# Two-layer masked attention: layer 1's q, k, v weights turned by VectorE instead of TensorE, with layer 1's features in another order

## The chip, the cores and the metric

The kernel runs on one core of a Trainium2 chip. The metric is device time in microseconds (us) for one whole execution. The profiles are single executions taken by the hardware profiler; in them PE is TensorE's matmuls, PEld its weight loads, DVE is VectorE, ACT ScalarE, POOL GpSimd, SP SyncE (which here issues all transfers), and L12 means line 12 of the kernel.

## The reference, cut to what matters

x is 128 x 128 x 512 in float32 (128 graphs of 128 nodes, 512 features), adj a boolean mask per graph. Two attention layers, each followed by a residual and a layer norm:

```python
# layer 0: 4 heads of 64
q, k, v = split_heads(x @ Wq), split_heads(x @ Wk), split_heads(x @ Wv)
sim = where(adj, q @ k.T * 64 ** -0.5, -max_float)
x = layernorm(x + softmax(sim) @ v @ Wo + bo)
# layer 1: 8 heads of 64
h = (x - mean) * rsqrt(var + 1e-5) * gamma + beta
q, k, v = split(h @ w_qkv.T)              # w_qkv is 1536 x 512
scores = where(adj | eye, q @ k.T * 64 ** -0.5, -1e9)
x = layernorm(x + softmax(scores) @ v @ w_out.T + b_out)
```

The weights of layer 0 are stored with the contracted feature as the row. w_qkv and w_out of layer 1 are stored with the output as the row, so that a matmul, which contracts over partitions, needs them turned.

## The kernel before

**Tiling.** Two graphs make a group g (G = 2); there are 64 groups. The 512 features are four chunks of 128 partitions (KC = 4). Every projection (layer 0's q, k, v; layer 1's qk and v; both output projections) is computed on 2 x 2 blocks with seven block products instead of eight, in the Strassen-Winograd manner; `product_0`, `product` and `out_product` issue them by number (1 to 7). The sums of blocks of x that this needs are made by GpSimd (`halves_sums`, L320), the sums of blocks of the weights once, in the opening and steps 2 to 4 (`combine`, L211: four subtractions, by VectorE except for one half of layer 1's qk). Products that share a PSUM bank must wait until ScalarE or VectorE has read the bank in between (the table `INTO`, L331; "a", "f" and "c" are the banks).

**Order.** The order of all instructions on each engine is written out by hand: `opening` (L804), `step(s)` for s = 2 to 63 (L846), then `closing_a`, `closing_b` twice, and `last`. Each engine takes its instructions in this order. Step s works on several groups at once: layer 0's projections of group s, layer 0's scores of s - 1, its attention and output of s - 2, layer 1's projections of s - 3, its scores of s - 4, its attention and output of s - 5.

**Transfers.** SyncE issues all transfers, in program order. x of a group comes in twice: as rows (`load_rows`, L83, the residual) and in column quarters (`load_quarters`, L99): quarter a holds features 128a to 128a + 127, goes to partitions 32a to 32a + 31, and a piece is 128 floats (512 bytes). `transposed` (L111) turns these by VectorE's transposes of 32 x 32 blocks, which leaves partition 32a + i of chunk c with feature 128a + 32c + i; layer 0's weights are loaded to match (L127 to L130, in quarters of 32 partitions, 1 KB pieces). Layer 1's input takes another way: `turn` (L246) transposes blocks of the normed rows, a trip through DRAM (`put`, `fetch`) moves blocks between partitions, and `finish` (L284) applies gamma and beta. The last two groups skip the trip: `finish_direct` (L299) turns their rows on TensorE.

**Layer 1's weights.** `load_transposed` (L147) loads a block r of 128 rows of w_qkv (12 blocks) or w_out (4) into a spare buffer of 128 partitions with 2 KB rows, and puts a function into the list `setup`. When called, it turns the block by four TensorE transposes into one PSUM bank, which ScalarE (odd r) or VectorE (even r) copies into w1 or wo1. `prepare(n)` (L800) calls the next n of the list: in the opening ten are called ahead of layer 1's first weight sums, two more later, and the rest (gamma and beta, w_out) in step 2. The spare buffers are two of the row buffers' pairs, KQ, v1, xT1 and aT1.

**The opening's order of transfers** is: x of group 0 in quarters (four transfers), Wk, Wq, Wv (four each), w_qkv blocks 0 to 3, x of group 1 (x_1) in quarters, mask 0, blocks 4 and 5, Wo, blocks 6 to 9, rows of group 0, bias 0, blocks 10 and 11, gamma, beta, w_out (four), rows and mask of group 1, bias 1, rows and mask of group 2, x of group 2 (x_2) in quarters.

**The opening's order of work** on TensorE is: layer 0's products of group 0 (1, 2, then 5, 6, 3, 7, 4), scores of group 0, products of group 1 (1, 2, 6, 5, 7), the transposes pt of group 0's probabilities (L649, `blocks_direct`), products 3 and 4 of group 1; then step 2 begins with scores of group 1, `attend` of group 0 (L677), and `product_0(2, 1)`, which reads x_2 turned. VectorE's own order between scores and pt is: turn x_1, mask the scores (L583), maxima (L589), the sums of w_out of layer 0 (`weight_sums_out(0)`, L221), the add of product 2 (L490), two of the weight blocks, the reciprocal (L606), on which GpSimd's product with the probabilities (L607) waits.

Of the kernel before, what the change touches and what calls it, by code (L numbers as in the profile page):

```python
# [10 lines left out]
F32 = mybir.dt.float32  # L11
U8 = mybir.dt.uint8  # L12
AF = mybir.ActivationFunctionType
ALU = mybir.AluOpType
# [3 lines left out]
P = 128  # L18
D = 64
G = 2  # L20
# [3 lines left out]
SCALE = D ** -0.5  # L24
# [3 lines left out]
def kernel(ctx: ExitStack, tc: tile.TileContext, x, adj, wq, wk, wv, wo, bo,  # L28
                            gamma, beta, w_qkv, w_out, b_out, out):
    nc = tc.nc  # L30
# [40 lines left out]
    K0, K1 = HEADS[0] // 2, HEADS[1] // 2  # L71
    KQ = const.tile([P, 4, 2, G, K1, 32], F32, name="kq")

    spare_rows(five, "r", 2)
    spare_rows(five, "r", 2)
    kq_rows = KQ.rearrange("p a w b c j -> p (a w b c j)")
    spare.extend(kq_rows[:, i * E:(i + 1) * E] for i in range(4))
    for pool, tag in ((two, "v1"), (two, "v1"), (one, "xT1"), (one, "aT1")):
        spare_rows(pool, tag, 2)

    X, XT = {}, {}

# [58 lines left out]
        nc.tensor.matmul(ready[:, :P], ident, ident, start=True, stop=True, skip_group_check=True)  # L141

    w1 = const.tile([P, KC, 3 * INNER[1]], F32, name="w1")
    wo1 = const.tile([P, INNER[1] // P, E], F32, name="wo1")
    setup = []

    def load_transposed(dst, src, name, *which):  # L147
# [12 lines left out]
        for r in which:  # L160
            raw = spare.pop(0)
            nc.sync.dma_start(raw, src[r * P:(r + 1) * P, :])
            setup.append(lambda r=r, raw=raw: part(r, raw))

    transposed(0)
    load_transposed(w1, w_qkv, "w_qkv", 0, 1, 2, 3)
    load_quarters(1)
    load_mask(0)
    load_transposed(w1, w_qkv, "w_qkv", 4, 5)
    wo0 = const.tile([P, INNER[0] // P, E], F32, name="wo0")  # L170
    nc.sync.dma_start(wo0, wo.rearrange("(c p) f -> p c f", p=P))
    load_transposed(w1, w_qkv, "w_qkv", 6, 7, 8, 9)
    load_rows(0)
    bias0 = const.tile([P, E], F32, name="bias0")
    nc.sync.dma_start(bias0, bo[None, :].to_broadcast([P, E]))
    load_transposed(w1, w_qkv, "w_qkv", 10, 11)
    gb_raw = one.tile([2 * KC, P], F32, tag="sm2", name="gb_raw")
    gb = const.tile([P, 2 * KC], F32, name="gb")
    nc.sync.dma_start(gb_raw[:KC], gamma.rearrange("(c p) -> c p", p=P))
    nc.sync.dma_start(gb_raw[KC:], beta.rearrange("(c p) -> c p", p=P))  # L180

    def turn_gamma_beta():
        pt = mm_tile("gb_t")
# [7 lines left out]
    bias1 = const.tile([P, E], F32, name="bias1")  # L191
    nc.sync.dma_start(bias1, b_out[None, :].to_broadcast([P, E]))

    I1 = INNER[1]
    KH = KC // 2

    w1qk = w1[:, :, :2 * I1].rearrange("p c (h f) -> p c h f", h=2)
    w1v = w1[:, :, 2 * I1:].rearrange("p c (h f) -> p c h f", h=2)
    wsqk = const.tile([P, 3, KH, I1], F32, name="wsqk")
    wsv = const.tile([P, 3, KH, I1 // 2], F32, name="wsv")  # L200

    def weight_sums(w, ws, *blocks_):

# [9 lines left out]
        for o, a, b in ((b12, b12, b11), (t2, b22, b12), (t3, t2, b11), (t4, b21, t2)):  # L213
            eng.tensor_tensor(o, a, b, op=ALU.subtract)  # L214

    def weight_sums_0(t):
        combine(*(w0[:, c:c + KH, t, h] for c in (0, KH) for h in range(2)), *(ws0[:, i, :, t] for i in range(3)))

    WSO = tuple(const.tile([P, 3, i // P // 2, E // 2], F32, name=f"wso{l}") for l, i in enumerate(INNER))

# [25 lines left out]
    def turn(g):  # L246
        if not 0 <= g < NG:
            return
        t = one.tile([P, 4, G * KC * 32], F32, tag="turned", bufs=2, name=f"turned_{g}")
        for b in range(G):  # L250
            nc.vector.transpose(t.rearrange("p a (b c i) -> p a b c i", b=G, c=KC)[:, :, b],
                                R[g][:, b].rearrange("p (c a i) -> p a c i", a=4, i=32))
        SCR[1] = put(t, f"scr_{g}")

    def arrive(g):
# [28 lines left out]
    def finish(g, half):  # L284
# [11 lines left out]
        if half == 1:  # L296
            sums(1, g)

    def finish_direct(g):  # L299

        xT = XT[1, g] = one.tile([P, KC, T], F32, tag="xT1", name=f"xT1_{g}")
        for b in range(G):
            pt = mm_tile(f"ht{g}_{b}")
            for c in range(KC):
                nc.tensor.transpose(pt[:, c * N:(c + 1) * N], R[g][:, b, c * P:(c + 1) * P], ident)
            for c in range(KC):
                o, i = xT[:, c, b * N:(b + 1) * N], pt[:, c * N:(c + 1) * N]
                scale, bias = gb[:, c:c + 1], gb[:, KC + c:KC + c + 1]
                if b == 0:
                    nc.scalar.activation(o, i, AF.Identity, bias=bias, scale=scale)  # L310
                else:
                    nc.vector.tensor_scalar(o, i, scale, bias, op0=ALU.mult, op1=ALU.add)
# [410 lines left out]
    def roots(l, g):  # L723
        mv = MV[l, g]
        if l == 0:


            ve1, root = power(l, g, mv[:, :, 1], 1, EPS * EPS, 1.0 + EPS)
        else:
            ve1, root = power(l, g, mv[:, :, 1], 1, EPS)  # L730
        shift = two.tile([P, G], F32, tag="shift", name=f"shift{l}_{g}")
        nc.gpsimd.tensor_tensor(shift, mv[:, :, 0], root, op=ALU.mult)
        nc.gpsimd.tensor_scalar_mul(shift, shift, -1.0)  # L733

        def ratios():

            ratio = RATIO[g] = three.tile([P, G], F32, tag="ratio", bufs=5, name=f"ratio_{g}")
            _, root0 = power(l, g, mv[:, :, 1], 0, EPS)
            nc.gpsimd.tensor_tensor(ratio, ve1, root, op=ALU.mult)
            nc.gpsimd.tensor_tensor(ratio, ratio, root0, op=ALU.mult)  # L740

        def norms():
            for b in range(G):
                nc.scalar.activation(R[g][:, b], R[g][:, b], AF.Identity, bias=shift[:, b:b + 1],  # L744
                                     scale=root[:, b:b + 1])
            if l == 1:
# [57 lines left out]
    def opening():  # L804

        sums(0, 0)
        cleared(1, 0)

        for t in (1, 0, 2):
            if t == 0:  # L810
                for h in range(2):
                    nc.vector.tensor_scalar_mul(w0[:, :, 0, h, :], w0[:, :, 0, h, :], SCALE)
            product_0(0, 1, 2, ts=(t,))
            weight_sums_0(t)
        product_0(0, 5, 6, 3)
# [24 lines left out]
        weight_sums(w1qk, wsqk, 0)  # L840
        product_0(1, 3)
        prepare(2)
        product_0(1, 4)
        transposed(2)

    def step(s):  # L846
# [18 lines left out]
            exps(s, 0, 0)  # L865
        product_0(s, 1)
        exps(s, 0, *((0, 1) if s < 5 else (1,)))
        out_product(0, s - 2, 1, 2, *(() if s == 2 else (5,)))
        maxima(s, 1 if s == 4 else 2)
        product_0(s, 2)  # L870
        if s == 2:
            out_product(0, s - 2, 5, 6)
        normalised(s, 0)
        out_product(0, s - 2, *(() if s == 2 else (6,)), 3)
        exps(s, 1, 0)
        if s == 4:
            maxima(s, 2)
# [274 lines left out]
```

## Time and profile before

| | us |
|---|---|
| median of three runs | 2735.53 (2735.45 to 2735.92) |
| the profiled execution | 2737.01 |
| its span in the profile | 2735.2 |
| TensorE busy | 2720.4 (99%) |
| VectorE busy | 2027.1 (74%) |
| GpSimd busy | 1750.5 (64%) |
| ScalarE busy | 1503.3 (55%) |
| the transpose of a weight block's copy: VectorE L158, mean | 0.683 |
| the same, ScalarE L156, mean | 0.581 |
| VectorE's transpose of 128 x 512 (L118), mean | 0.686 |
| x_2's transfers, issue to landing | 6.5 to 8.0 |

The profiled execution is 1.8 us longer than its span, which is what lies ahead of the first and behind the last instruction. "Busy" is the time in which at least one instruction of the engine was under way. A row of a timeline gives start, length, engine, line, operation, output and inputs; a bracket behind it gives the time that the engine had stood idle and what ended it. The chain of waits follows, from the last instruction back, what released each one.

### The profile page before, as it was taken

Reading aid. Unit: us, or ns where it says so; the run is one execution under the profiler, and the core shown is the slowest. Engines: PE = TensorE matmul, PEld = TensorE weight load, DVE = VectorE, ACT = ScalarE, POOL = GpSimd, SP = SyncE. Lnnn points to the kernel's source line nnn. Section 1 sums busy time; section 2 is a strip of 40 time slices with the busy share of each in tenths; the row PEclk is TensorE's granted clock in tenths of the full one; section 3 lists DMA queues with packets and bytes.
Section 4 is the critical chain, followed back from the end, with each engine's and each line's share of the span. In section 5 each row is a group of like instructions: output and inputs, shape, how many; then the busy total and the mean of one; then the engine's idle time right before and its main releaser. Section 6 shows DMA issues by size and latency. Waiting matters only on the chain.

```text
span 2735.2 us, 47645 instructions
## 1 busy us (share of the span) xinstructions
PE 2720.4 (99%) x14943; PEld 1933.5 (71%) x14943; DVE 2027.1 (74%) x3671; ACT 1503.3 (55%) x4804; POOL 1750.5 (64%) x2311
## 2 busy tenths in 40 slices
PE   9999999999999999999999999999999999999999
PEld 8867767667677676676776766767767667677688
DVE  6777777777777777777777777777777777777765
ACT  3456465465564554655646546556465465564654
POOL 5575666666766656667566666676666666756664
PEclk9999999999999999999999999999999999999999
DMA  6567777777777777777777777777777777777742
GB/s 180 156 204 207 218 221 206 219 214 219 211 208 218 220 200 217 214 215 211 208 222 217 206 220 213 216 215 205 216 220 206 220 214 217 209 208 222 207 142 70
DMA packets 550283, 562.62 MB, mean 206 GB/s; under 512 B 55560, under 2 KB 468752, under 8 KB 550032
## 3 DMA queue, kind: packets, MB, share of 16 engines
q1 hardware_dynamic: 550032, 559.58, 71.9%
q8 instruction: 121, 1.98, 0.3%
q14 instruction: 130, 1.06, 0.1%
HBM read 300.95 MB, written 258.47 MB: 205 GB/s over the span
## 4 chain that ended last, share of the span: by engine, by line
PE 96%; DMA 2%; SPq 1%; ACT 0%; issue 0%; DVE 0%; POOL 0%; POOLq 0%; ACTq 0%; DVEq 0%
PE qka L363 16%; PE a L476 12%; PE oa L514 11%; PE qkf L363 8%; PE va L363 8%; PE av L677 6%; PE f L476 6%; PE of L514 6%; PE qkc L363 4%; PE vf L363 4%; PE c L476 3%; PE oc L514 3%; PE sc L548 2%; PE sc L554 2%; PE vc L363 2%; PE sc_a L554 2%
## 5 line engine op out<-in xcount | busy, mean ns | idle before, releaser
L598 ACT ACTIVATE sm<-sm,nmax 128x128 f32<-128x128 f32 x1536 | 595.0, 393 | 1.6 <-DVE nmax L589 1.2
L607 POOL TENSOR_TENSOR sm<-sm,rec 128x1024 f32<-128x1024 f32 x192 | 364.1, 1897 | 340.8 <-DVE rec L606 337.4
L699 POOL TENSOR_TENSOR r<-r,bias 128x1024 f32<-128x1024 f32 x128 | 301.2, 2354 | 128.3 <-ACT r L698 128.3
L518 DVE TENSOR_TENSOR r<-oa,r 128x256 f32<-128x256 f32 x508 | 212.1, 417 | 161.6 <-PE oa L514 124.9
L598 ACT ACTIVATION_READ_ACCUMULATOR sm<-sm,nmax 128x1 f32 x1536 | 294.7, 192 | 0.0
L373 ACT COPY ev<-va 128x256 f32<-128x256 f32 x128 | 47.6, 372 | 432.5 <-PE va L363 432.5
L625 DVE STREAM_TRANSPOSE turnedp<-sm 128x1024 f32<-128x1024 f32 x188 | 233.4, 1242 | 62.4 <-POOL sm L607 57.9
L718 POOL TENSOR_SCALAR ve<-mv 128x2 f32<-128x2 f32 x191 | 41.4, 217 | 370.7 <-DVE mv L711 360.2
L744 ACT ACTIVATE r<-r,shift,root 128x512 f32<-128x512 f32 x254 | 193.0, 808 | 87.8 <-POOL shift L733 87.8
L589 DVE TENSOR_REDUCE nmax<-sm 128x8 f32<-128x1024 f32 x192 | 226.7, 1207 | 0.3
L363 PE MATMUL qkf<-w,xs 128*128 128x512 f32 x472 | 221.8, 592 | 0.0
L363 PE MATMUL qka<-wsqk,xs 128*128 128x512 f32 x472 | 221.8, 592 | 0.0
L514 PE MATMUL of<-wo,so 128*128 128x256 f32 x760 | 205.7, 379 | 0.3 <-DVE r L518 0.3
L514 PE MATMUL oa<-wso,so 128*128 128x256 f32 x760 | 205.6, 379 | 0.0
L326 POOL TENSOR_TENSOR xs<-xT 128x256 f32<-128x256 f32 x256 | 188.1, 735 | 24.3 <-DVE xT L118 19.8
L428 ACT ACTIVATE qo<-kq 128x512 f32<-128x512 f32 x118 | 67.9, 622 | 227.9 <-DMA kq<-scrkq 227.9
L476 PE MATMUL f<-w,xs 128*128 128x384 f32 (+1 forms) x512 | 181.1, 476 | 0.2 <-DVE w L214 0.2
L476 PE MATMUL a<-ws,xs 128*128 128x384 f32 (+1 forms) x512 | 181.0, 476 | 0.0
L583 DVE COPY_PREDICATED sm<-m,sc 128x512 f32<-128x512 uint8 x256 | 172.6, 728 | 11.2 <-PE sc L548 2.6
L710 DVE BATCH_NORM_STATS2 st<-r 128x6 f32<-128x512 f32 x254 | 174.9, 689 | 2.2
L569 POOL MEMSET sm<- 128x1024 f32 x192 | 175.1, 951 | 1.4 <-DVE turnedp L625 1.4
L514 PEld LDWEIGHTS oa<-wso,so 128*128 128x128 f32 x760 | 143.7, 190 | 45.7 <-issue 0.7
(181 smaller groups left out, 6340.3 us busy)
## 6 DMA issues: line engine op xcount, KB each, us to landing
scrp<-turnedp SPq DMA_DIRECT2D x188, 512.0 KB, 3.5
pT<-scrp SPq DMA_DIRECT2D x752, 128.0 KB, 2.9
kq<-scrkq SPq DMA_DIRECT2D x236, 256.0 KB, 4.8
x<-in_x_dram SPq DMA_DIRECT2D x256, 128.0 KB, 3.9
r<-in_x_dram SPq DMA_DIRECT2D x64, 512.0 KB, 4.2
out_dram<-r SPq DMA_DIRECT2D x63, 512.0 KB, 3.6
scr<-turned SPq DMA_DIRECT2D x62, 512.0 KB, 6.7
kq<-scr SPq DMA_DIRECT2D x248, 128.0 KB, 2.8
```

The source lines that it names most:

```text
L326: nc.gpsimd.tensor_tensor(o, a0, a1, op=op)
L363: nc.tensor.matmul(o, lhsT, rhs, start=first and m == 0, stop=m == len(todo) - 1, skip_group_check=True)
L476: nc.tensor.matmul(o, lhsT, rhs, start=first and n == 0, stop=n == len(todo) - 1, skip_group_check=True)
L514: nc.tensor.matmul(acc, left[:, c], right[:, c], start=first and c == 0, stop=c == hk - 1, skip_group_check=True)
L518: nc.vector.tensor_add(part, acc, part)
L569: nc.gpsimd.memset(sm, NEG1 if part else NEG0)
L589: nc.vector.tensor_reduce(NMAX[part], SM[part], AX.X, ALU.max, negate=True)
L598: nc.scalar.activation(sm[:, i, k, :], sm[:, i, k, :], AF.Exp, bias=nmax[:, i, k:k + 1], accum_out=total[:, i, k:k + 1])
L607: nc.gpsimd.tensor_tensor(SM[part], SM[part], rec[:, :, :, None].to_broadcast([P, 2, K1, N]), op=ALU.mult)
L625: nc.vector.transpose(t.rearrange("p q (h r) -> p q h r", r=32), SM.pop(part).rearrange("p i k (q r) -> p q (i k) r", r=32))
L699: nc.gpsimd.tensor_tensor(R[g], R[g], (bias0, bias1)[l][:, None, :].to_broadcast([P, G, E]), op=ALU.add)
L744: nc.scalar.activation(R[g][:, b], R[g][:, b], AF.Identity, bias=shift[:, b:b + 1], scale=root[:, b:b + 1])
```

## The change

It has four parts.

- **w_qkv** is loaded in column quarters, as x is: `load_blocks` issues four transfers for a range of blocks, each to 32 partitions in pieces of 128 floats, and VectorE turns each block with one transpose instruction straight into w1. Blocks 0 to 3 come into KQ, 4 to 9 (before wo0) into the place of the weight sums wsqk, 10 and 11 into that of wsv. w_out is loaded and turned as before.
- **Layer 1's features** take the order that this leaves: partition 32a + i of chunk c holds feature 128a + 32c + i. `turn`, gamma and beta, and `finish_direct` follow; the latter reads a copy by chunks that ScalarE makes (`by_chunk`) right after the norm of the last two groups.
- **The opening's weight sums of layer 0** are issued one by one: of each four, those that the next product needs come first, and the scaling of Wq is moved ahead of the last two sums of Wk's.
- **Step 2** issues layer 0's output products in the order that the later steps have.

```diff
-    spare_rows(five, "r", 2)
-    spare_rows(five, "r", 2)
-    kq_rows = KQ.rearrange("p a w b c j -> p (a w b c j)")
-    spare.extend(kq_rows[:, i * E:(i + 1) * E] for i in range(4))
-    for pool, tag in ((two, "v1"), (two, "v1"), (one, "xT1"), (one, "aT1")):
-        spare_rows(pool, tag, 2)
+    for _ in range(2):
+        spare_rows(two, "v1", 2)
...
+    def load_blocks(home, lo, hi):
+
+        n = (hi - lo) * P // 32
+        raw = home[:, :n * P].rearrange("p (m f) -> p m f", f=P)
+        rows = w_qkv[lo * P:hi * P].rearrange("(m j) (a f) -> a j m f", j=32, a=4)
+        for a in range(4):
+            nc.sync.dma_start(raw[32 * a:32 * a + 32], rows[a])
+
+        def part(r):
+            nc.vector.transpose(w1[:, :, r * P:(r + 1) * P].rearrange("p c (m j) -> p m c j", j=32),
+                                raw[:, (r - lo) * 4:(r - lo + 1) * 4].rearrange("p m (c i) -> p m c i", i=32))
+
+        setup.extend(lambda r=r: part(r) for r in range(lo, hi))
+
     transposed(0)
-    load_transposed(w1, w_qkv, "w_qkv", 0, 1, 2, 3)
+    load_blocks(KQ.rearrange("p a w b c j -> p (a w b c j)"), 0, 4)
     load_quarters(1)
     load_mask(0)
-    load_transposed(w1, w_qkv, "w_qkv", 4, 5)
+    load_blocks(wsqk.rearrange("p i c f -> p (i c f)"), 4, 10)
     wo0 = const.tile([P, INNER[0] // P, E], F32, name="wo0")
     nc.sync.dma_start(wo0, wo.rearrange("(c p) f -> p c f", p=P))
-    load_transposed(w1, w_qkv, "w_qkv", 6, 7, 8, 9)
     load_rows(0)
     bias0 = const.tile([P, E], F32, name="bias0")
     nc.sync.dma_start(bias0, bo[None, :].to_broadcast([P, E]))
-    load_transposed(w1, w_qkv, "w_qkv", 10, 11)
+    load_blocks(wsv.rearrange("p i c f -> p (i c f)"), 10, 12)
...
-    nc.sync.dma_start(gb_raw[:KC], gamma.rearrange("(c p) -> c p", p=P))
-    nc.sync.dma_start(gb_raw[KC:], beta.rearrange("(c p) -> c p", p=P))
+    for i, of_feature in enumerate((gamma, beta)):
+        nc.sync.dma_start(gb_raw[i * KC:(i + 1) * KC].rearrange("c (a i) -> c a i", i=32),
+                          of_feature.rearrange("(a c i) -> c a i", a=4, i=32))
...
-    def weight_sums_0(t):
-        combine(*(w0[:, c:c + KH, t, h] for c in (0, KH) for h in range(2)), *(ws0[:, i, :, t] for i in range(3)))
+    def weight_sums_0(*which):
+
+        for t, i in which:
+            b11, b12, b21, b22 = (w0[:, c:c + KH, t, h] for c in (0, KH) for h in range(2))
+            t2, t3, t4 = (ws0[:, j, :, t] for j in range(3))
+            o, a, b = ((b12, b12, b11), (t2, b22, b12), (t3, t2, b11), (t4, b21, t2))[i]
+            nc.vector.tensor_tensor(o, a, b, op=ALU.subtract)
...
             nc.vector.transpose(t.rearrange("p a (b c i) -> p a b c i", b=G, c=KC)[:, :, b],
-                                R[g][:, b].rearrange("p (c a i) -> p a c i", a=4, i=32))
+                                R[g][:, b].rearrange("p (a c i) -> p a c i", a=4, i=32))
...
+    def by_chunk(g, b):
+
+        if b == 0:
+            BY_CHUNK[g] = one.tile([P, G, KC, P], F32, tag="xT0", name=f"by_chunk_{g}")
+        nc.scalar.copy(BY_CHUNK[g][:, b].rearrange("p c (a i) -> p a c i", i=32),
+                       R[g][:, b].rearrange("p (a c i) -> p a c i", a=4, i=32))
...
-                nc.tensor.transpose(pt[:, c * N:(c + 1) * N], R[g][:, b, c * P:(c + 1) * P], ident)
+                nc.tensor.transpose(pt[:, c * N:(c + 1) * N], BY_CHUNK[g][:, b, c], ident)
...
+            if l == 0 and g >= NG - 2:
+                for b in range(G):
+                    by_chunk(g, b)
...
-        for t in (1, 0, 2):
-            if t == 0:
-                for h in range(2):
-                    nc.vector.tensor_scalar_mul(w0[:, :, 0, h, :], w0[:, :, 0, h, :], SCALE)
-            product_0(0, 1, 2, ts=(t,))
-            weight_sums_0(t)
+        product_0(0, 1, 2, ts=(1,))
+        weight_sums_0((1, 0), (1, 1))
+        for h in range(2):
+            nc.vector.tensor_scalar_mul(w0[:, :, 0, h, :], w0[:, :, 0, h, :], SCALE)
+        product_0(0, 1, 2, ts=(0,))
+        weight_sums_0((0, 0), (2, 0))
+        product_0(0, 1, 2, ts=(2,))
+        weight_sums_0((0, 1), (2, 1), (1, 2), (0, 2), (2, 2), (1, 3), (0, 3), (2, 3))
         product_0(0, 5, 6, 3)
...
-        out_product(0, s - 2, 1, 2, *(() if s == 2 else (5,)))
+        out_product(0, s - 2, 1, 2, 5)
         maxima(s, 1 if s == 4 else 2)
         product_0(s, 2)
-        if s == 2:
-            out_product(0, s - 2, 5, 6)
         normalised(s, 0)
-        out_product(0, s - 2, *(() if s == 2 else (6,)), 3)
+        out_product(0, s - 2, 6, 3)
```

More of the change, by code (lines that the diff above doesn't have):

```diff
@@ L143 @@
     w1 = const.tile([P, KC, 3 * INNER[1]], F32, name="w1")
+    I1 = INNER[1]
+    KH = KC // 2
+    wsqk = const.tile([P, 3, KH, I1], F32, name="wsqk")
+    wsv = const.tile([P, 3, KH, I1 // 2], F32, name="wsv")
     wo1 = const.tile([P, INNER[1] // P, E], F32, name="wo1")
@@ L192 @@
     nc.sync.dma_start(bias1, b_out[None, :].to_broadcast([P, E]))
-    I1 = INNER[1]
-    KH = KC // 2
     w1qk = w1[:, :, :2 * I1].rearrange("p c (h f) -> p c h f", h=2)
     w1v = w1[:, :, 2 * I1:].rearrange("p c (h f) -> p c h f", h=2)
-    wsqk = const.tile([P, 3, KH, I1], F32, name="wsqk")
-    wsv = const.tile([P, 3, KH, I1 // 2], F32, name="wsv")
     def weight_sums(w, ws, *blocks_):
@@ L297, in finish @@
             sums(1, g)
+    BY_CHUNK = {}
+    def by_chunk(g, b):
[3 more added lines that the diff above has]
+                       R[g][:, b].rearrange("p (a c i) -> p a c i", a=4, i=32))
     def finish_direct(g):
```

## The prediction

> **What bounds the kernel now.** I read the page first (busy shares, chain of waits), then the chain and the VectorE timeline of the first 45 us, then a table of stretches for the transfers, then SyncE's waits.
>
> ```profile
> PE 2720.4 (99%) x14943; PEld 1933.5 (71%) x14943; DVE 2027.1 (74%) x3671; ACT 1503.3 (55%) x4804; POOL 1750.5 (64%) x2311
> PE 96%; DMA 2%; SPq 1%; ACT 0%; issue 0%; DVE 0%; POOL 0%; POOLq 0%; ACTq 0%; DVEq 0%
> ```
>
> TensorE is busy in 99% of the span and makes 96% of the chain: whatever it gains or loses in the opening stays to the end. From 16 us on the opening's chain has no gap:
>
> ```profile
> 23.73 1.28 PE sc L548 x16
> ...
> 27.88 0.87 PE w_qkvt L152 x8
> ...
> 34.52 0.87 PE pt L649 x8
> ...
> 40.23 1.02 PE av L677 x16
> 41.26 1.55 PE a L476 x12
> ```
>
> (start, length, what.) Each block of weights that TensorE turns (L152) costs eight records and 0.87 us on the chain for two blocks. So TensorE looks like the bound here. But look at who only just arrives:
>
> ```profile
> 27.62 0.42 DVE L214 TENSOR_TENSOR wo<-wo 128x256 f32<-128x256 f32 x1
> 39.36 1.30 DVE L118 STREAM_TRANSPOSE xT<-x 128x512 f32<-128x512 f32 x2 [1.43 <-DMA x<-in_x_dram]
> ```
>
> Group 2's x is turned at 39.36, after VectorE had stood 1.43 us waiting for its transfer; it ends at 40.66, and product_0(2, 1), which reads it, starts at 41.2. TensorE has 0.5 us of slack against a transfer at the tail of the opening's queue. That queue is full:
>
> ```profile
> 5.00:11.50 6.50, 2.71 (x21) 2.36 (x21) 5.02 (x8) 0.00 (x0) 3.98 (x5) 0.97 1.11 227
> 11.75:14.50 2.75, 2.75 (x15) 2.75 (x14) 1.40 (x4) 0.30 (x1) 0.00 (x0) 0.51 1.04 371
> 14.75:17.30 2.55, 2.39 (x21) 2.20 (x20) 2.08 (x5) 0.48 (x1) 0.00 (x0) 1.00 1.22 193
> 17.50:28.50 11.00, 11.00 (x104) 10.63 (x104) 6.92 (x11) 3.31 (x9) 3.04 (x4) 1.00 1.04 381
> 28.50:38.50 10.00, 10.00 (x93) 10.00 (x92) 6.13 (x12) 5.94 (x21) 7.24 (x6) 1.00 0.83 203
> SPq L162 <- DMA r<-in_x_dram: 2.3, 1, 2.3
> ```
>
> (stretch, length, five engines' busy us, granted clock, DMA share, GB/s; last line from SyncE's waits.) The share is above 1 until 28.5 us. The rate goes by the form of the load: w0 in 32-partition quarters 227 GB/s, x_1 in quarters of 512-byte pieces (with a mask) 193, loads of 128 partitions with 2 KB rows 371 to 381. SyncE holds each transfer until the eighth before it has landed (the last line: w_out's third block waited for row tile 0, eight earlier), so x_2, the 48th to 51st, can't overtake.
>
> **What the skill says.** The Trainium skill, "SBUF — State Buffer", Door 1: The DMA port swizzle: partitions 0 to 31 reach 8 of the 16 ports; it gives 189 GB/s at 1 MiB with a limit near 218, against 328 and 436 for 128 partitions. The trace agrees: 193 to 227 against 371 to 381. "DMA: Bandwidth & Descriptors", Specifications, puts the smallest piece for line rate at 512 B, so it would see no loss from the pieces alone; here piece and quarter come together, and the measured quarter rate is used. "TensorE: Matmul & The Clock Gate", Part 1, says that idle time halves the clock until some 3.4 us of work have passed; the trace agrees: after the gap that ends at 11.2 the granted clock is 0.5 until 14.3, which cost about 1.65 us.
>
> **The change, part by part** (profiled execution: span 2735.2, its own time 2737.0; the median of the runs is 2735.5, and I add the difference to that).
>
> *TensorE's transposes go*: six pairs at 0.87, -5.2 us. Their copies (VectorE six at 0.68, ACT six at 0.58) go too; twelve VectorE transposes of 128x512 come, at 0.69 by the L118 row: VectorE +4.1 us net. They lie on VectorE's in-order queue between work that TensorE waits for: beside r0, r1 the add of product 7, which gates product 4 (0.6 to 1.2 us of TensorE waiting), and r4, r5 ahead of L606's reciprocal.
>
> *Opening's sums*: the scaling of Wq starts when Wq lands (9.9) instead of after four sums (10.6), -0.7; product 5 no longer waits for the sums of v, -0.4. Together -1.1.
>
> Without transfers in the way TensorE would finish scores(1) at 23.4 (before 25.0). The next chain is maxima, w_out's sums, the add, two transposes, reciprocal, GpSimd's product: 25.95 + 2.1 + 0.56 + 1.4 + 0.2 + 1.9 = 32.1 for the transposes pt (before 34.4), and 37.7 at the end of attend(2) (before 41.2): -3.5 us at most, since VectorE's chain takes the rest.
>
> *The transfers*: 3.15 MB of w_qkv change from rows to quarters. At 381 GB/s they took 8.3 us. At 215, between the two quarter rates seen, they take 14.6: +6.4 us of a full queue (ends: 245, the best that a quarter load of x shows later, +4.6; 193, +8.0; a gain is excluded, since no quarter load in the trace reaches the row rate). Blocks 6 to 9 also move ahead of wo0, row tile 0 and bias0 on SyncE's queue. Number and order are otherwise kept (twelve transfers before and after), so issue time is unchanged.
> - Queue from 11.7: blocks 0-3 to 16.6, x_1 and mask 19.4, blocks 4-9 26.7, wo0 28.1, landed about 28.6 (before 20.5). VectorE reaches w_out's sums at 25.95 and stands 2.6 us; behind it stand the add of product 2, r4, r5 and the reciprocal, and so GpSimd's product and pt: 28.6 + 2.1 + 0.56 + 1.4 + 0.2 + 1.9 = 34.7. The whole gain of TensorE is gone at pt, and attend(2) ends at 40.6.
> - x_2 landed at 39.3; +6.4 makes 45.7. From 28.5 to 38.5 the share is 0.83, so some of that slack may close: I take 0.7 (0 to 2.5). Landed at 45.0, turned by 46.3: TensorE starts product_0(2, 1) 5.1 us later than before.
> - TensorE stands some 5 us ahead of it; the clock falls as it did at 11 us: +1.65 (0 to 1.65).
>
> *Step 2's order*: product 3 no longer waits for the add of product 5 in the same bank: -0.3, the one idle place there.
>
> *Feature order*: turn, finish and the product keep their instructions and shapes: nothing; their cover is that only the strides differ. Loading gamma and beta in smaller pieces: 4 KB, nothing.
>
> *by_chunk*: four ACT copies of 128x512 at about 0.55. The pair for group 62 falls where ACT next idles 3 us: nothing, or 0.3 through the exponentials. The pair for group 63 stands ahead of the copy of v's product 6:
>
> ```profile
> 2677.09 0.37 ACT L373 COPY ev<-va 128x256 f32<-128x256 f32 x1
> 2677.69 1.03 PE L363 MATMUL va<-wsv,xs 128*128 128x256 f32 x4
> ```
>
> The copy ends 0.2 us before product 7 writes the same bank; 1.1 us later it costs +0.85 (0 to 1.2).
>
> Sum: +5.1 + 1.65 - 0.3 + 0.85 = +7.3, so 2742.8. The saved 5.2 and 1.1 don't appear: they lie ahead of x_2's arrival and are spent waiting for it.
>
> **Rivals.**
> *A, the forecast*: the quarter loads fill the queue longer and x_2 sets the end of the opening. For it: shares above 1, two quarter rates, VectorE's 1.43 us. Own range: +4.6 - 2.5 lands x_2 at 41.4, TensorE +1.5, no clock loss, +0.55: 2737.5. Top: +8.0 and no slack, +7.4 + 1.65 + 0.9: 2745.5. Chance 0.70.
> *B, x_2 arrives when it did*: the slack behind 28.5 us takes up all of it. TensorE waits until 40.65: -0.5, +0.55 closing, clock 0 to 1.6: about 2736.0. Against it: the share before 28.5 leaves no slack there, so at most 2.5 of 4.6 close. Chance 0.16.
> *C, not slower*: x_2's landing is set by SyncE's hold on issue and not by bytes. Its place is the stretch behind 28.5, where the share falls below 1; if the transfers there start earlier and x_2 is in by 36.4, VectorE's chain sets the end: -3.5 - 0.3 + 0.85, 2732.6. It decides at 39.9: landing later than that, TensorE gains nothing. If VectorE's chain gave way too, -5.2 - 1.1 - 0.3 + 0.85 = -5.75, 2729.8. Against it: the hold itself waits for landings. Chance 0.14, of which 0.05 below 2730.
>
> **From the numbers.** 0.2% is 5.5 us, about what a measurement of this kernel can tell from no change: slower means above 2741.0. Of A's 0.70, 0.55 lies there, since the middle of each term gives more; 0.15 below. Same: 0.15 + 0.16 + 0.09 = 0.40. Faster 0.05. The range runs from 2734.0, which leaves out most of C (0.12), to 2745.5, which leaves out A's upper end (0.05); A alone is 2737.5 to 2745.5.
>
> **What would show it.** Right: a DMA rate near 215 from 12 to 17 and from 19 to 27 us, w_out's sums on VectorE waiting for wo0 until about 28, the transpose of x_2 waiting for its transfer until about 45 (before 39.4), a TensorE gap of several us ahead of product_0(2, 1) with the clock at 0.5 behind it, and some 0.8 us at 2678. Wrong: w_qkv's transfers at 300 GB/s or more, x_2 turned at 40 or earlier, no gap ahead of product_0(2, 1), or a loss in the steady steps, where I expect none.

## The result, and the profile after

| | before, us | after, us |
|---|---|---|
| median of 6 runs each, side by side | 2735.49 (2734.16 to 2736.50) | 2745.27 (2744.55 to 2747.20) |
| ratio, 95% interval | 1 | 1.0037 (1.0026 to 1.0048) |
| the profiled execution; its span | 2737.01; 2735.2 | 2745.31; 2743.5 |

The change makes the kernel slower by 0.37%, 9.8 us between the medians. Between the two profiled executions it is 8.3 us. TensorE's timeline of the changed kernel (start, length, engine, line, what, and in brackets the idle time ahead and its releaser):

```profile
36.52 1.97 PE L672 MATMUL pt<-ident,sm 128*128 128x128 f32 x8 [4.68 <-POOL sm L630]
48.86 2.07 PE L499 MATMUL a<-xT,w 128*128 128x128 f32 x8 [4.97 <-DVE xT L114]
58.84 1.04 PE L672 MATMUL pt<-ident,sm 128*128 128x128 f32 x8
```

The first row is pt, the turn of group 0's probabilities (34.4 before), the second product_0(2, 1), the third the next pt, that of group 1. The last two in the kernel before, with no idle time ahead:

```profile
41.19 1.16 PE L476 MATMUL a<-xT,w 128*128 128x128 f32 x8
49.75 1.04 PE L649 MATMUL pt<-ident,sm 128*128 128x128 f32 x8
```

(The expectations further down number attends, masks and turns by the step that issues them: their attend of group 2 is the attend that step 2 issues, of group 0, and their turn of group 2's probabilities is the next pt, of group 1.) VectorE's timeline shows whom TensorE waited for:

```profile
31.04 0.42 DVE L223 TENSOR_TENSOR wo<-wo 128x256 f32<-128x256 f32 x1 [4.58 <-DMA wo<-in_L_gnn_Wo_dram]
48.09 1.30 DVE L114 STREAM_TRANSPOSE xT<-x 128x512 f32<-128x512 f32 x2 [6.05 <-DMA x<-in_x_dram]
```

The sums on Wo start 3.4 us later than before (27.62), the turn of x_2 8.7 us later (39.36). The chain of waits, which before ran through TensorE here, now runs through transfers:

```profile
26.20 9.98 DMA wsv<-in_L_gnn_w_qkv_dram
...
36.20 6.50 DMA r<-in_x_dram
...
42.72 5.16 DMA x<-in_x_dram
```

The stretches (start and end, length, busy us of five engines, granted clock, DMA share, GB/s):

```profile
17.00:19.50 2.50, 2.50 (x25) 2.50 (x24) 0.88 (x2) 0.48 (x1) 0.00 (x0) 1.00 1.23 201
19.50:27.00 7.50, 6.47 (x61) 5.92 (x60) 6.38 (x10) 1.40 (x5) 2.77 (x4) 1.00 1.19 191
...
48.00:54.00 6.00, 5.14 (x23) 4.80 (x24) 4.88 (x8) 2.12 (x10) 2.88 (x4) 0.59 0.37 93
```

```profile
33.00:34.00 1.00, 0.00 (x0) 0.00 (x0) 1.00 (x3) 0.00 (x0) 0.00 (x0) 1.00 0.21 36
34.00:35.00 1.00, 0.00 (x0) 0.00 (x0) 1.00 (x4) 0.00 (x0) 0.44 (x1) 1.00 0.35 73
```

Three things to see: the quarters of blocks 4 to 9 move at 191 GB/s; the clock is 0.59 behind the gap; and from 33 to 35 us the queue is nearly empty (before: 314 and 222 GB/s) while x_2 isn't even issued (SyncE issues its first quarter at 38.71 and its last at 42.72, before at 29.93 and 32.65). The trace's record of landings explains the third. A transfer lands in 16 parts; here are the 15th and the last of them, in us:

```
                            before            after
last load of blocks 4-9     23.14  23.19      27.69  29.53
Wo                          20.42  20.48      29.13  31.02
rows of group 0             24.54  25.88      30.74  33.60
bias 0                      25.20  26.57      31.91  34.69
```

Fifteen parts are there, and the last comes 1.3 to 1.4 us behind them in the kernel before (the last two rows; the first two landed ahead of the lag), 1.7 to 2.9 us in the changed one. The lag begins with the first transfer to land after the instruction queue has moved a 16 KB packet (at 23.53, for 1.13 us, before; at 22.60, for 1.36 us, after), which makes the packet a suspect; the last section has a run that speaks against it as the only cause. SyncE issues a transfer only when the eighth before it has landed whole, and w_out's first block went out at 33.61, as the last part of the rows of group 0 came in, 2.9 us behind the other fifteen.

Where the 8.3 us between the profiles lie, by the starts of the same instructions: product_0(2, 1) +7.67; from there to the next pt +1.42 (9.98 against 8.56); from the first product of layer 1 (80.89) to the attend at 2619.76 -0.8; the next 35 us of the closing -0.8 (two waits of before, 0.29 us for ScalarE's qo and 0.49 for its xT, aren't there); v's products of the last group but one +0.9 (by_chunk). The steady steps differ by up to 4 us between the executions profiled here (2536.7 to 2540.4 us for the same stretch), so small effects below are read from the opening and the closing and not from the total.

### The profile page after: what moved, and what is told of

It reads as the page before. It is cut to its first block, busy times and chain, and to the rows that moved or that the text cites. A ratio compares the mean times of both kernels' runs of the same rounds, so it can differ in the third digit from the quotient of the medians.

```text
span 2743.5 us, 47544 instructions
## 1 busy us (share of the span) xinstructions
PE 2719.8 (99%) x14895; PEld 1932.8 (70%) x14895; DVE 2030.0 (74%) x3677; ACT 1503.0 (55%) x4802; POOL 1753.1 (64%) x2311
## 4 chain that ended last, share of the span: by engine, by line
PE 96%; DMA 2%; SPq 1%; ACT 0%; DVE 0%; issue 0%; POOL 0%; POOLq 0%; DVEq 0%; ACTq 0%
PE qka L386 16%; PE a L499 12%; PE oa L537 12%; PE qkf L386 8%; PE va L386 8%; PE av L700 6%; PE f L499 6%; PE of L537 6%; PE qkc L386 4%; PE vf L386 4%; PE oc L537 3%; PE c L499 3%; PE sc L571 2%; PE sc L577 2%; PE vc L386 2%; PE sc_a L577 2%
```

## The experiments

Theory: x_2's late arrival sets the end of the opening, the transfers over 32 partitions make it late, and the clock halves in the wait. Times are medians; before stood at 2734.9 to 2736.2 beside each.

**What makes the loads slow.** Three kernels change only the form of layer 1's twelve transfers; their w1 holds the weights in a wrong order, the work is the same.

```diff
-        rows = w_qkv[lo*P:hi*P].rearrange("(m j) (a f) -> a j m f", j=32, a=4)
+        rows = w_qkv[lo*P:hi*P].rearrange("(a m j) f -> a j m f", j=32, a=4)    # p32_2k: 32 partitions, 2 KB
+        rows = w_qkv[lo*P:hi*P].rearrange("(m j) (a f) -> a j m f", j=P, a=4)   # p128_512: 128 partitions, 512 B
+        rows = [r for h in w_qkv[lo*P:hi*P].rearrange("(h m j) (b f) -> h b j m f", j=P, b=2, h=2) for r in h]   # p128_1k: 128 partitions, 1 KB
...
```

> The changed kernel with layer 1's twelve transfers each over 32 partitions as before, but in whole rows of 2 KB in place of pieces of 512 B (so w1 holds its rows in a wrong order: other numbers, same work). In the changed kernel the first four (kq, 256 KB each) land 1.15 us apart, 228 GB/s, and blocks 4 to 9 at 192 to 206 GB/s. Theory 'few partitions': still 1.1 to 1.3 us apart, x of group 2 turned near 48 us, product 1 and 2 of group 2 at 48 to 49.5 us, time 2744 to 2747. Rival 'small pieces': 0.65 to 0.75 us apart as the rows before (0.68), x of group 2 turned by 41 us, time under 2739.

> The same twelve transfers with 512 B pieces of the same column quarters, but each spread over all 128 partitions (w1's order is again wrong, the work is the same). Theory 'few partitions': kq's four land 0.65 to 0.8 us apart, and x of group 2 is turned 6 us earlier than in the changed kernel (42 us or before). Rival 'small pieces' (or reads of one column quarter crowding the memory): 1.1 us apart or more, nothing gained.

> The same twelve transfers over 128 partitions in pieces of 1 KB (w1's order wrong, work the same): what the change would do if its transfers were as fast as rows. Theory (bytes per second and the hold behind them are the whole loss): kq's four 0.7 us apart, x of group 2 arrives about as before, product 1 of group 2 starts at 38 to 41.5 us, and the time falls to 2733 to 2737 us, level with before or up to 0.1% under it. Rival (the loss is in the turns on VectorE or elsewhere in the change): 2741 or more.

Blocks 0 to 3 (four transfers of 256 KB), the mean from landing to landing, by the same records:

```
form                      us each   GB/s   x_2's turn starts   time, us
32 partitions, 512 B        1.15     228        48.09           2745.27 (the change)
32 partitions, 2 KB         1.22     215        47.30           2741.96 (one run)
128 partitions, 512 B       0.92     286        42.73           2740.15 (one run)
128 partitions, 1 KB        0.78     338        40.97           2738.64
128 partitions, 2 KB        0.76     345        39.36           2735.17 (before)
```

The 32 partitions are what slows them: whole rows over 32 partitions are no faster, 512 B pieces over 128 are. (1.15 and 1.22 us don't differ: the changed kernel's quarters took 1.22 to 1.25 us in x2_early, wo_early and best, 210 to 215 GB/s.) That agrees with the Trainium skill, "SBUF — State Buffer", Door 1, though 228 is a little above the limit of 218 given there. The piece counts too, which "DMA: Bandwidth & Descriptors", Specifications, would not have it (full rate from 512 B): 286 at 512 B, 338 at 1 KB; the measurement decides. (Between 1 and 2 KB the means hardly differ; the kernel before took 0.68, 0.68 and 0.92 us.) p128_512 was thus slower than the 0.65 to 0.8 us expected, and its x_2 came at 42.73 and not by 42. The lag of the last part stayed at 1.3 to 1.4 us in both kernels over 128 partitions. p32_2k's time is under its band, though x_2 came as expected: its steady steps ran 2.2 us shorter than the changed kernel's.

p128_1k took 6.6 us off the changed kernel, by the form of the loads alone, but stayed above its theory: 1.0010 (1.0004 to 1.0017), 2738.6 and not 2733 to 2737, and under the rival's 2741. Its stretches:

```profile
36.00:42.00 6.00, 1.51 (x21) 1.15 (x20) 1.03 (x2) 0.59 (x1) 5.11 (x7) 0.85 0.58 113
42.00:48.00 6.00, 6.00 (x27) 5.46 (x28) 4.00 (x7) 3.25 (x16) 2.86 (x4) 0.58 0.40 93
```

TensorE, 5 us of transposes lighter, finishes attend at 37.2 and then stands 4.49 us, because x_2 comes no earlier than before (it lands at 40.74, before at 39.14); behind that the clock is 0.58 and the stretch to the next pt takes 10.60 us against 8.56. Faster loads alone turn the saving into a longer wait and then into a slower clock.

> The changed kernel with quarters 2 and 3 of blocks 0 to 3 issued by ScalarE, so that transfers of two partition quarters can run at once. Theory (32 partitions take 215 to 228 GB/s, whoever else runs; two quarters at once reach more): the four land within 3.2 to 4 us of the last w_v in place of 5.1 us. Rival (one queue's order isn't the limit; the engines are): 4.8 us or more.

```diff
-            nc.sync.dma_start(raw[32 * a:32 * a + 32], rows[a])
+            (nc.scalar if lo == 0 and a > 1 else nc.sync).dma_start(raw[32 * a:32 * a + 32], rows[a])
```

2745.65 in one run. ScalarE issued its two quarters at 1.33 and 4.04 us, so they ran among the loads of x and of layer 0's weights and not behind the last of Wv, and the 3.2 to 4 us expected can't be read. The rate was 220 and 229 GB/s while both queues ran (before, with one queue, 225 to 231). Two queues didn't gain; what within the transfer is the limit stays open.

**Whether x_2 sets the end.**

> The changed kernel with x of group 2 sent for right behind Wo of layer 0 (its own buffer), ahead of residual, bias and blocks 10 and 11, all else as it is. Theory (x of group 2 is the wait that sets the end, and the stall on Wo costs only while that wait is gone): VectorE turns it before attend of group 2 ends, product 1 of group 2 starts at 43.5 to 45 us in place of 48.86, time 2740 to 2742. Rival (the wait on x stands for others that come as late: residual, blocks 10 and 11, output weights): 47.5 us or later, 2744 to 2746.

```diff
+    x_2 = five.tile([P, BB, E // 4], F32, tag="r", name="x_2")     # shortened: four quarters into it, issued behind Wo
...
         transposed(1)
-        load_quarters(2)
+        X[0] = x_2
```

> The changed kernel with Wo of layer 0 sent for ahead of blocks 4 to 9. Theory (x of group 2 sets the end; what VectorE waited for on Wo it then waits for on the blocks, and TensorE only idles longer before x): the 4.58 us stall on Wo is gone, product 1 of group 2 still starts at 48 to 49.5 us, time 2744.5 to 2747. Rival (the stall on Wo is itself part of the loss): 2740 to 2742.

```diff
+    nc.sync.dma_start(wo0, wo.rearrange("(c p) f -> p c f", p=P))
     load_blocks(wsqk.rearrange("p i c f -> p (i c f)"), 4, 10)
-    nc.sync.dma_start(wo0, wo.rearrange("(c p) f -> p c f", p=P))
```

x2_early: 2740.21, 1.0019 (1.0012 to 1.0026), 5.1 us under the changed kernel. TensorE's timeline:

```profile
37.82 1.97 PE L682 MATMUL pt<-ident,sm 128*128 128x128 f32 x8 [5.60 <-POOL sm L640]
46.13 1.16 PE L509 MATMUL a<-xT,w 128*128 128x128 f32 x8
54.18 1.04 PE L682 MATMUL pt<-ident,sm 128*128 128x128 f32 x8
```

No gap ahead of product_0(2, 1), and 8.05 us to the next pt. It starts later than the 43.5 to 45 expected: Wo lands 1.3 us later still, and half the clock lasts until 42.66 us behind the wait for it. wo_early: 2745.59, 1.0037 (1.0023 to 1.0050), no gain at all. Its rows:

```profile
34.75 1.09 PE L672 MATMUL pt<-ident,sm 128*128 128x128 f32 x8 [2.45 <-POOL sm L630]
48.43 2.08 PE L499 MATMUL a<-xT,w 128*128 128x128 f32 x8 [5.98 <-DVE xT L114]
```

pt is 1.8 us earlier, and TensorE waits a microsecond longer for x_2. Taking away the first of two stalls in a row gives nothing; taking away the last gives 5 us.

**Whether the clock's loss is real.**

> The changed kernel with 30 matmuls of 128x128 that nobody reads (some 4 us at full clock) behind attend of group 2, where TensorE otherwise waits 4.97 us for x of group 2. In the changed kernel the stretch from product 1 of group 2 to the turn of its probabilities takes 9.98 us, in the kernel before 8.56. Theory (half of the clock is lost behind that idle time): product 1 still starts at 48 to 49.5 us, the stretch falls to 8.0 to 8.6 us, time 2742.5 to 2744.5. Rival (the stretch is long for another reason, such as late residuals or masks): 9.5 us or more, time as the changed kernel or over it.

> As clock_fill with 19 matmuls in place of 30: there the 30 took 6.7 us, ended 2.1 us too late, and the stretch behind them was 7.95 us in place of 9.98; 19 take 4.3 us and end before x of group 2 is turned. Theory (about half of the clock over some 4 us, lost behind the idle time): product 1 of group 2 at 48.3 to 49.3 us, the stretch to the turn of its probabilities 7.9 to 8.4 us, time 2743 to 2744.5, that is 1 to 2 us under the changed kernel. Rival (the stretch was short only because its start was late): 9 us or more, 2745 to 2746.

```diff
         attend(s)
+        if s == 2:
+            fill = mm_tile("fill")
+            for _ in range(30):                                      # clock_fill_19: 19
+                nc.tensor.matmul(fill[:, :P], ident, ident, start=True, stop=True, ...)
```

With 30, the stretch fell from 9.98 to 7.95 us at a granted clock of 1.00 from 48 to 54 us, but the filler itself ran 2.1 us past x_2: 2745.93. With 19, product_0(2, 1) started at 49.08, the next pt came 1.0 us earlier than in the changed kernel, and the time was 2744.31, 1.0029 (1.0018 to 1.0041), as expected. The stretch was 8.79, above the theory's 8.4 and under the rival's 9: at the full clock TensorE waits within it for VectorE, which is late with x_2 as well (0.47 us idle from 54 to 60 us), so about 1.2 of the 2 us is to be had.

The trace's record of the clock shows the loss itself. The half clock comes in pieces of 3.41 or 6.83 us (in the changed kernel 46.06 to 52.89 us), and what a wait costs is half of the part of the piece that falls into the work behind it. Without any, the stretch from product_0(2, 1) to the next pt takes 8.06 us with this order of step 2 (sums_only below):

```
run           piece of half clock   product_0(2, 1)   half of it in the stretch   stretch less 8.06
changed       46.06 to 52.89        48.86             2.0                         1.9
pool_copy     48.75 to 52.17        48.43             1.7                         1.6
p32_2k        47.88 to 51.29        48.06             1.6                         1.5
wo_early      46.26 to 53.09        48.43             2.3                         2.2
p128_1k       40.19 to 47.02        41.73             2.6                         2.5
p128_512      42.08 to 48.91        43.49             2.7                         2.6
two_queues    47.75 to 54.58        48.49             3.0                         2.9
x2_early      none there            46.13             0                           0.0
```

**What by_chunk costs.**

> The changed kernel with by_chunk on GpSimd in place of ScalarE, nothing else. Theory (by_chunk on ScalarE costs 0.9 us near the end, and the best run's lower end came from it): the stretch from the last steady step to layer 1's last products shrinks from 68.98 to about 68.05 us, time 2743.9 to 2745. Rival (GpSimd's copy becomes the wait in its place): no shorter, 2745 to 2746.

```diff
-        nc.scalar.copy(BY_CHUNK[g][:, b]...
+        nc.gpsimd.tensor_copy(BY_CHUNK[g][:, b]...
```

TensorE's timeline, first of the changed kernel, then of pool_copy:

```profile
2683.42 1.03 PE L386 MATMUL va<-wsv,xs 128*128 128x256 f32 x4
2685.95 1.13 PE L386 MATMUL va<-wsv,xs 128*128 128x256 f32 x4 [0.64 <-ACT ev L396]
```

```profile
2682.78 1.03 PE L386 MATMUL va<-wsv,xs 128*128 128x256 f32 x4
2684.51 1.03 PE L386 MATMUL va<-wsv,xs 128*128 128x256 f32 x4
```

The stretch from the attend at 2619.76 (pool_copy: 2619.16) to layer 1's last products shrank from 68.98 to 68.04 us: by_chunk on ScalarE costs 0.9. The time, 2744.45, 1.0029 (1.0019 to 1.0040), fits.

**What the sums are worth alone**, from the kernel before:

> The kernel before with the reordered sums of the opening and of step 2 alone, transfers and turns as they were. Theory (TensorE is busy throughout the opening and x of group 2 lands at 39.3 us whatever VectorE does): product 1 of group 2 starts at 40.7 to 41.5 us, time 2733.5 to 2736, within 0.1% of before. Rival (the sums are the good half of the change, worth over 2 us that the late transfers hid): 2733 or less.

> The kernel before with the reordered sums of the opening and of step 2, and x of group 2 sent for behind blocks 6 to 9 in its own buffer; layer 1's weights still by whole rows and TensorE. Theory (TensorE, busy 12 of 12 us from 30 to 42 us, is the bound there, and x had only 0.5 us of slack to give): product 1 of group 2 starts at 40 to 41 us, time 2733.5 to 2735.5, 0 to 2 us under before. Rival (the sums gain on their own what the forecast gave them, and more, once x is no limit): 2732 or less.

The edits are the diff's parts on `weight_sums_0`, `opening`'s first products and `out_product` in step 2; sums_x2 adds x_2's early load. sums_only: 2735.28, 0.9997 (0.9989 to 1.0005). sums_x2: 2733.80, 0.9993 (0.9985 to 1.0001). Neither can be told from no change. The stretch from product_0(2, 1) to the next pt is 8.06 and 8.05 us, before 8.56: step 2's order gives 0.5. In the opening both missed: product_0(2, 1) started at 43.02 (expected 40.7 to 41.5) and 42.23 (40 to 41), later than before, with TensorE busy 6.00 of 6 us from 18 to 54 us. Their profiled executions had 6.83 us of half clock there (11.98 to 18.81 and 10.64 to 17.47), before's had 3.41 (11.05 to 14.46), which is some 1.5 us more lost; in sums_only the last quarter of Wv landed 1.1 us late as well. So the profiles don't show what the opening's sums are worth, and the times show nothing measurable.

**Putting it right, with the loads as they are.**

> The changed kernel with three moves: Wo ahead of blocks 4 to 9, x of group 2 right behind them in its own buffer, and the copy by_chunk on GpSimd. Theory (two late landings and the clock lost behind them are the loss): VectorE now waits some 2 to 3 us for blocks 4 to 9 in place of Wo, attend of group 2 ends at 41.5 to 44 us, product 1 follows with no idle time and the clock stays full, by_chunk's 0.9 us at the end is gone: 2735.5 to 2738. Rival (the change costs elsewhere too): 2740 or more.

> The kernel of the run best (Wo ahead, x of group 2 early, by_chunk on GpSimd) with the masks of groups 1 and 2 right behind x of group 2. Theory (VectorE's 2.23 us wait for that mask, and TensorE's 2.12 us behind it, go): the turn of group 2's probabilities at 51.3 to 52.5 us (best 54.02, before 49.75), time 2735.5 to 2737.5. Rival (residual of group 0 or blocks 10 and 11 take its place): 53.5 us or later, 2738 or more.

> As the run before, and the turns of blocks 4 to 9 stand behind the attend of group 1 and the layer-1 sums on GpSimd behind the sums of group 2, so that nothing in the opening's chain waits for a block of layer 1 above 3. Theory: no VectorE stall, attend of group 2 ends at 37 to 38.5 us, product 1 of group 2 starts at 37.5 to 40 us (before: 41.19), time 2731.5 to 2734.5, which is under the kernel before. Rival (x of group 2 still lands at 39 us or later, behind 6.5 MB of loads): product 1 at 40.5 to 42 us, 2735 to 2738.

> The kernel of the run late_turns with the masks of groups 1 and 2 (32 KB each) right behind x of group 2; there VectorE waited 4.55 us for the mask of group 2. Theory (once x is early the mask behind the residual is the next late transfer, and nothing else is): that wait is gone, product 1 of group 2 still at 38 to 39 us, the turn of group 2's probabilities at 47.5 to 49.5 us (before 49.75, late_turns 52.47), time 2735 to 2737.5. Rival (the next late transfer, the residual of group 0 or blocks 10 and 11, takes its place): 51 us or later, 2739 or more.

> The kernel of the run late_masks with the layer-1 sums on GpSimd behind group 2's normalising in place of ahead of it (there TensorE waited 3.39 us for that). Theory (the change's saving on TensorE is real once nothing in the opening waits for a late transfer): product 1 of group 2 at 38 to 39 us, the turn of its probabilities at 46.5 to 49 us (before 49.75), time 2731.5 to 2735. Rival (the opening has no slack for the turns on VectorE and the sums on GpSimd, wherever they stand): 50 us or later, or the loss comes back within step 2; 2736 or more.

The edits are those above together, and `load_mask(1)` and `load_mask(2)` behind x_2 (best_masks and the two late_masks runs), and for the late runs the following, with the line marked "to step 2" put behind the sums of group 2 in late_turns and late_masks, behind the last normalising of step 2 in late_masks_2:

```diff
         exps(1, 0, 0, 1)
-        prepare(2)
         normalised(1, 0)
         product_0(1, 6, 5)
-        prepare(2)
...
-        prepare(2)
         blocks_direct(1, 0)
         cleared(2, 0)
-        weight_sums(w1qk, wsqk, 0)                  # to step 2
+        prepare(2)
         product_0(1, 3)
...
         transposed(2)
+        prepare(2)
```

| run | product_0(2, 1) | next pt | first product of layer 1 | time | ratio |
|---|---|---|---|---|---|
| before | 41.19 | 49.75 | 71.80 | | 1 |
| changed | 48.86 | 58.84 | 80.89 | 2745.27 | 1.0037 |
| best | 41.93 | 54.02 | 76.06 | 2738.25 | 1.0011 (1.0004 to 1.0018) |
| best_masks | 42.37 | 52.49 | 74.59 | 2739.01 | 1.0010 (1.0002 to 1.0018) |
| late_turns | 38.35 | 52.47 | 75.85 | 2740.20 | 1.0019 (1.0012 to 1.0026) |
| late_masks | 38.26 | 52.50 | 78.86 | 2741.83 | 1.0020 (1.0014 to 1.0027) |
| late_masks_2 | 38.49 | 49.26 | 75.01 | 2739.29 | 1.0010 (1.0003 to 1.0016) |

best is 0.25 us above its 2738, and TensorE still stood 0.92 us ahead of product_0(2, 1). Each removal uncovers the next wait. In best it is VectorE's, for the mask of group 1 behind the rows (it lands at 44.57; the expectations call it group 2's):

```profile
44.70 1.34 DVE L616 COPY_PREDICATED sm<-m,sc 128x512 f32<-128x512 uint8 x2 [2.23 <-DMA m<-in_adj_dram]
```

In late_turns the same wait is 4.55 us. With the masks early it is gone, and GpSimd's 5 us of layer-1 sums become the wait: in late_masks TensorE stands 3.39 us behind them, and in late_masks_2, where they come later, VectorE does, in step 3:

```profile
61.55 1.35 DVE L619 COPY_PREDICATED sm<-m,sc 128x512 f32<-128x512 uint8 x2 [2.97 <-POOL sm L605]
```

So these expectations were too low, each by the wait that they did not name: best_masks by 1.5 us, late_turns by 5.7, late_masks and late_masks_2 by 4.3. For late_masks_2 the rival held: from the next pt to the first product of layer 1 it takes 25.75 us, before 22.05, a third of that loss at the end of step 2 (two waits of 0.68 us for ScalarE's copies of w_out), the rest in step 3. best_masks' gain at the next pt (1.5 us over best) doesn't show in its time.

**Whether the saving exists.**

> The kernel of the run p128_1k (layer 1's weights over 128 partitions in 1 KB pieces, so in a wrong order in w1, work the same) with x of group 2 and the masks of groups 1 and 2 behind Wo, and by_chunk on GpSimd. Theory (the design is sound and only its transfers are late): attend of group 2 ends at 37 to 38.5 us, product 1 follows with no idle time at 37.5 to 39.5 us (before 41.19), the first product of layer 1 at 68.5 to 71 us (before 71.80), time 2731.5 to 2735, under before. Rival (TensorE's saved 5.2 us come back as waits for VectorE and GpSimd within step 2, as in late_masks_2): the first product of layer 1 at 72 us or later, 2736 or more.

2731.78, 0.9991 (0.9983 to 0.9999), under the kernel before. TensorE's timeline, then its stretches:

```profile
38.59 1.16 PE L513 MATMUL a<-xT,w 128*128 128x128 f32 x8
47.68 1.09 PE L686 MATMUL pt<-ident,sm 128*128 128x128 f32 x8
...
69.78 1.95 PE L400 MATMUL qka<-xT,w 128*128 128x128 f32 x16
```

```profile
36.00:42.00 6.00, 5.70 (x55) 4.66 (x54) 5.32 (x9) 2.77 (x10) 5.69 (x7) 1.00 1.04 247
42.00:48.00 6.00, 5.93 (x46) 5.27 (x45) 3.11 (x8) 2.53 (x12) 5.47 (x7) 1.00 0.18 38
```

With transfers over 128 partitions and x_2 early, product_0(2, 1) starts 2.6 us before its old place, at full clock, and the first product of layer 1 2.0 us before. This kernel's weights are in the wrong order, so it isn't a version to use. Its time is 3 us under the kernel before measured beside it, as expected, which p128_1k (fast loads, late x_2) and best_masks (slow loads, early x_2) each fail to reach alone.

Two things keep this from showing that the turns on VectorE are what saves. This profiled execution had no half clock in its opening, before's had 3.41 us; without these, before's product_0(2, 1) would have started at about 40.1 us, when x_2's first half is turned, so some 1.1 of the 2.6 us are not the kernel's doing (an estimate, from 39.36 and the 0.77 us between the turn's start and the product's in the changed kernel). And the kernel before gains as well from an early x_2 and the new order of sums: sums_x2 stands at 0.9993 (0.9985 to 1.0001), and the two intervals overlap. What the turns on VectorE save beyond that is not shown.

## Why the prediction was right or wrong

- **What sets the end of the opening**: right. x_2's arrival does, with a gap ahead of product_0(2, 1) and the half clock behind it (x2_early, wo_early). The saved transposes and sums don't appear, as said.
- **Transfers up to Wo**: right for the bulk. Blocks 0 to 3 ended at 16.7 (said 16.6), x_1 and the mask at 19.3 (19.4), Wo's bulk at 28.84 (28.6). Its last part came at 31.02, so pt was at 36.5 and not 34.7; that cost nothing, x_2 being later.
- **x_2's delay: the step that failed.** "Number and order are otherwise kept (twelve transfers before and after), so issue time is unchanged", and of the slack behind 28.5 us "I take 0.7". The term was +5.1 and measured +7.67; x_2 landed at 47.87 and not at 45.0. Three things made the difference. Blocks 4 to 9 moved at 191 GB/s, not 215 (8.2 us instead of 7.3): with the other blocks, the bulk of w_qkv's last load came 7.6 us later than before and not 6.4, +1.2. Its last part, which the hold waits for, came 8.8 us later, another +1.2: with that part up to 2.9 us late, SyncE stood and the queue ran at 36 and 73 GB/s from 33 to 35 us. And none of the slack closed: x_2's landing was 8.7 us later. I had listed the hold as a reason for a gain (rival C); it is a second loss. Against this, half a microsecond was hidden by a reading that was wrong: product_0(2, 1) needs only the first half of x_2 turned (it starts at 48.86, the turns end at 49.39), so TensorE's slack was 1.1 us and not 0.5. The rate is shown by the runs on the form of the load; the lag's part is read from the trace and wasn't undone by a run of its own.
- **The clock**: right in kind, +1.65 (0 to 1.65) said. Against sums_only (8.06 us with the same order of step 2) the stretch is 1.9 longer: the piece of half clock was 6.83 us and not 3.4, and 4.0 us of it fell into the work. Step 2's order gave 0.5, not 0.3.
- **by_chunk**: +0.85 said, 0.9 shown by pool_copy.
- **Steady steps**: no loss expected, and none came; -0.8 there, inside what one execution differs from the next, and -0.8 in the closing, which the sum did not have. These two hid 1.6 us of the loss in the profiled execution, which is luck.
- **Rivals.** B didn't occur. p128_1k is the nearest to it: x_2 was turned 1.6 us later than before, and the clock's price was 2.5 us (10.60 against 8.06), above the 0 to 1.6 allowed. C's mechanism didn't occur in the change, but its end, VectorE's chain at 37.7 with nothing late, is what p128_x2_early has (attend ends at 38.6).
- **The number**: by the profiles +7.3 stood against +8.3; the medians are another 1.5 us apart, because before's profiled execution lay above its median (2737.01 against 2735.5) and the changed kernel's did not. The time, 2745.27, lies at the range's upper end of 2745.5, and the ratio's interval (2742.6 to 2748.6 on 2735.5) reaches past it. That end gave x_2's delay 8.0 us with no slack, and no room for a queue that runs empty.

## What to carry to other kernels

When an edit slows transfers, follow the queue to its end: in these kernels the issue of a transfer hangs on the last part of one eight places ahead, so slow loads not only push the later ones back, they can let the queue run dry. Work saved ahead of a late arrival is worth nothing, and in p128_1k it was worth less than nothing, since the longer wait brought the half clock behind it. Before two profiles are compared by their start times, compare their clocks: here two openings can differ by up to 3.4 us through that alone (half of 6.83 us). Change the order of loads first, by when each is read, and count every load that the next step reads, small masks too.

## What the runs showed of the hardware that was not expected

- One of the 16 parts in which a transfer lands falls behind by 0.9 to 1.8 us and stays behind for many transfers. In 18 of the 19 profiles this begins with the first transfer to land after a 16 KB instruction packet (moved at 20.9 to 25.3 us, in 1.1 to 1.5 us). In sums_only it begins at 13.19 us, nine us ahead of that packet, so the packet isn't the only cause. In p128_512 and p128_1k the lag stays at 1.3 to 1.4 us; it grew to 2.9 in the changed kernel, to 2.3 in x2_early, to 2.0 in best, and to 3.1 in p128_x2_early, where the loads ahead went over 128 partitions. Why it begins and grows stays open.
- Over 128 partitions, pieces of 512 B, 1 KB and 2 KB moved at 286, 338 and 345 GB/s in the same place; over 32 partitions 512 B at 210 to 228 and 2 KB at 215.
- The half clock came in pieces of 3.41 or 6.83 us, and a wait cost half of what of the piece fell into the work behind it: 1.5 to 2.9 us in seven runs, within 0.2 us of the reckoning in each. Waits well under 3.41 us stood ahead of it too (2.38 us, ending at 11.23, in the kernel before; 2.12 us in best). Nearly the same wait in the opening (2.38, 2.49 and 2.50 us in before, sums_only and p128_x2_early) was followed by 3.41 us, 6.83 us and none.
